# Layer 0 of a four-layer convolution chain: one entry for three 64x64 matmul steps, and the planned order made anew

## The chip, the cores and the metric

The kernel runs on one core of a Trainium2 chip. The metric is device time in microseconds (us) of one execution; of several runs the median is given.

## The reference, cut to what matters

An input of 8 images, 128 channels, 96x96, passes four layers, each of the form x = x + conv(group_norm(x)). Only layer 0 is touched here, a deformable convolution:

```python
def _dcnv4_forward(x, dw_w, dw_b, gn_w, gn_b, om_w, om_b):
    x1 = depthwise 3x3 convolution of x + dw_b
    x1 = gelu(normalised over the image, gn_w, gn_b)
    om = einsum('nhwc,oc->nhwo', x1, om_w) + om_b     # 8 groups x 9 taps x (2 offsets, 1 mask)
    ...
    # each of 9 taps per group is read bilinearly at its offset place, times its mask
    out = jnp.sum(samp * mask[..., None], axis=4)
...
x = x + _L0_conv_ref(_gn(x), ...)      # layer 0
x = x + _L1_conv_ref(_gn(x), ...)      # 3x3
x = x + _L2_conv_ref(_gn(x), ...)      # depthwise with signs
x = x + _L3_conv_ref(_gn(x), ...)      # a scan over rows
```

## The kernel before, in words

**Work of layer 0.** An image is cut into BR = 6 chunks of 16 rows, so there are 48 chunks. A chunk's result is the sum of 25 shifted copies of the normalised image, each times a weight map. For each shift VectorE (DVE) multiplies a map row by a shifted slice (`pr`, line 1077), and TensorE (PE) adds the product into PSUM `ps_s` with 16 matmuls on 32x32 tiles (`add_all`, line 1031). From chunk 6 on one product in 25 is made by GpSimd (POOL, line 1085), in the last chunk seven. There are three `pr` buffers: product k+3 can't start before the add of product k has read its own. After 25 adds ScalarE (ACT) moves `ps_s` out (`y`, line 1111), and the first add of the next chunk (the residual, `sdd`) waits for that, as there is one `ps_s`.

**The weight maps.** POOL builds them per chunk into `wx` (lines 978 to 1012, two buffers) from "tents", ten ACT instructions on the offsets `om` (lines 943 to 952). ACT copies five rows of `wx` per chunk to PSUM for DVE (`ps_wb`, line 1054, two buffers of five products each). `om` comes from DRAM into one buffer (SP, line 922), after four projections on PE (line 899, `project`, two matmuls each into the one PSUM buffer `ps_w`), their evictions on ACT (`oe`, line 907) and their stores (line 915). A chunk's projections run some three chunks ahead, on x1 after GELU (`x1c`, line 884, loaded at line 880).

**The image ahead.** While the chunks of image i run, image i+1 is prepared: rows loaded (SP, line 502), statistics on ACT (line 604), a chain of tiny operations on DVE, PE and ACT for the group norm (lines 638 to 343), normalising on ACT (line 711), copies to DRAM (line 722), and the depthwise convolution in 12 blocks on PE. A block is three `near` taps (line 745, four 64x64 matmuls each) and three `over` taps (line 761, eight 32x32 matmuls each) into `ps_w`; ACT evicts it (line 783) and takes a square sum (line 790), SP stores it (line 799). After the 12th block a second chain of tiny operations (lines 813 to 837) gives the coefficients of the GELU, so the first projections of the next image wait for it.

**What sets the order.** The program has no dynamic order: all of it is planned in Python. Each piece is a `plan.task(engine, cost, fn, deps, prio, ...)`. `Plan.order` plays the engines against each other with the given costs, always starting the ready task of lowest `prio`, and each engine then issues its instructions in that fixed sequence. A cost, a prio or a constant has no other effect than on this sequence. `CH` is the spacing of the chunks' prios, `SLOT_AT` how early slices are loaded, `BEHIND1` how far image 1's preparation is put back, `EACH_ON_POOL` which product POOL makes, `STATS_LATE` an offset of the statistics.

Of the kernel before, what the change touches and what calls it, by code (L numbers as in the profile page):

```python
# [51 lines left out]
    return sorted(every, key=lambda s: (s[0] % NR, s[1] % NR))  # L52


CONV_COST = 0.66, 0.8
CH, SHIFT, PE_KEEP = 47.0, 8.6, 2.0
LOAD_AT, NORM_AT, COPY_AT, COPY_LATE, COPY_FROM = -140, -90, -20, 220, 52
CONV_AT, CONV_STEP, CONV_PACE = -60, 20, 1.5
X1_AT, OM_STEP, SLOT_AT = -140, 4.0, 35
BEHIND, AHEAD, CONV_BEHIND = 40, 60, 40  # L60
HOLD, BEHIND1 = False, 40
GATE, SLOTS_FROM = 12, 0
LAST_ON_POOL, EACH_ON_POOL, POOL_W = (4, 7, 10, 13, 16, 19, 22), (16,), 20
PAIR, FROM_CHUNK = 1, 6
STATS_ON_ACT, STATS_LATE = True, 0


class Buf:
# [136 lines left out]
def kernel(  # L205
# [33 lines left out]
    NB, HC = 2, P // 2  # L239
    YB, BR = 16, H // 16  # L240

    NQ, QC = 4, P // 4
# [186 lines left out]
    with ExitStack() as ph:  # L429
# [49 lines left out]
        plan = Plan()  # L479
# [95 lines left out]
        def image(i, at, before=()):  # L575
# [36 lines left out]
            prev = []  # L612
# [122 lines left out]
            for c in range(NST):  # L735
                ps = plan.buf("s" if i == 0 and c % 2 else "w")
                need = (norms[: NB * (c + 2)] if c < NST - 1 else norms) + (ready if i == 0 else [])
                prev = []

                def near(t, ps=ps, c=c):  # L740

                    r0, c0 = RP + c * RB, RS - 1 + t
                    for j in range(NB):
                        for h in range(2):
                            nc.tensor.matmul(
                                ps.tile[half(j), h, :FB],
                                dwn[half(h), j, t].rearrange("p e c -> p (e c)"),
                                xq[half(h), r0 : r0 + RB, j, c0 : c0 + W],
                                start=(t == 0),
                                stop=False,  # L750
                            )

                def over(t, ps=ps, c=c):

                    c0 = RS - 1 + t
                    for j in range(NB):
                        for p in range(2):
                            r0 = RP + c * RB + 1 - 2 * p
                            for h in range(2):
                                of = quarter(2 * h + p)  # L760
                                nc.tensor.matmul(  # L761
                                    ps.tile[quarter(2 * j + 1 - p), h, :FB],
                                    dwo[of, j, t],
                                    xq[of, r0 : r0 + RB, j, c0 : c0 + W],
                                    start=False,
                                    stop=(t == 2),
                                )

                when = at + CONV_AT + CONV_STEP * c
                for k in range(6):  # L770
                    prev = [task(
                        "PE", CONV_COST[k // 3], lambda t=k % 3, tap=(near, over)[k // 3]: tap(t), need + prev,
                        when + CONV_PACE * k + (CONV_BEHIND - BEHIND if i else 0), uses=[ps], lag=0.5,
                        shape=HC if k < 3 else QC,
                    )]
                for k in (c - 1, c, c + 1):
                    if (i, k) in free_rows:
                        free_rows[i, k] = free_rows[i, k] + prev
                x1 = plan.buf("x1")

                def evict(c=c, x1=x1, ps=ps):
                    for h in range(2):
                        nc.scalar.activation(
                            x1.tile[:, h, :], ps.tile[:, h, :FB], AF.Identity, accum_out=st1[:, h, c : c + 1]
                        )

                ev = plan.task("ACT", 1.5, evict, prev, when + 16 - AHEAD, uses=[ps, x1])
                stats1.append(plan.task(
                    "ACT", 0.97,
                    lambda c=c, x1=x1: nc.scalar.activation(  # L790
                        junk[:], x1.tile[:], AF.Square, accum_out=st1[:, 2, c : c + 1]
                    ),
                    [ev], when + 18, uses=[x1],
                ))

                def store(c=c, x1=x1):
                    for j in range(NB):
                        for p in range(2):
                            nc.sync.dma_start(
                                x1d[i, j, p].rearrange("(h c) k w -> c h (k w)", h=2)[:, :, c * FB : (c + 1) * FB],  # L800
                                x1.tile[quarter(2 * j + p), :, :],
                            )

                outs.append(plan.task("SP", 2.4, store, [ev], when + 18, uses=[x1], lag=2.2, move=1.3))
# [66 lines left out]
        def chunk(i, dy, made):  # L871
# [177 lines left out]
            for sy in range(NS):  # L1049
                wb = plan.buf("wb")  # L1050
                d, y = places[sy]
                cp = plan.task(
                    "ACT", 0.62,
                    lambda wb=wb, d=d, y=y: nc.scalar.activation(  # L1054
                        wb.tile[:, : NS * W], wx.tile[:, d, y].rearrange("p x w -> p (x w)"), AF.Identity
                    ),
                    known[sy], at + SHIFT * (sy - 1) - AHEAD, uses=[wb, wx], lag=0.1,
                )
                slot = slots[dy + sy]
                last_chunk = n == N * BR - 1  # L1060
                on_pool_k = LAST_ON_POOL if last_chunk else EACH_ON_POOL if n >= FROM_CHUNK else ()
                sx = 0
                while sx < NS:
                    shared = k in on_pool_k
                    m = PAIR if not shared and sx + PAIR <= NS and not any(k + e in on_pool_k for e in range(PAIR)) else 1
                    pr = plan.buf(("oe" if last_chunk else "oe") if shared else "pr")
                    when = at + SHIFT * sy + SHIFT / NS * sx

                    def mul(wb=wb, pr=pr, slot=slot, sx=sx, m=m):
                        rows = slot.tile[:, :, sx : sx + W]  # L1070
                        parts, *free = rows.ap
                        nc.vector.tensor_tensor(
                            pr.tile[:, :m],
                            wb.tile[:, sx * W : (sx + m) * W].rearrange("p (s w) -> p s w", s=m).unsqueeze(2).to_broadcast([P, m, GC, W]),
                            bass.AP(rows.tensor, rows.offset, [parts, [1, m], *free]),
                            ALU.mult,
                        ) if m > 1 else nc.vector.tensor_tensor(  # L1077
                            pr.tile[:, 0],
                            wb.tile[:, sx * W : (sx + 1) * W].unsqueeze(1).to_broadcast([P, GC, W]),
                            rows,  # L1080
                            ALU.mult,
                        )

                    def mul_pool(pr=pr, slot=slot, sx=sx, d=d, y=y):
                        nc.gpsimd.tensor_tensor(
                            pr.tile[:],
                            wx.tile[:, d, y, sx].unsqueeze(1).to_broadcast([P, GC, W]),
                            slot.tile[:, :, sx : sx + W],
                            ALU.mult,
                        )  # L1090

                    if shared:
                        t = plan.task("POOL", 3.65, mul_pool, [*known[sy], slot.load], when - POOL_W, uses=[wx, pr, slot], lag=0.1)
                    else:
                        t = plan.task("DVE", 0.06 + 1.66 * m, mul, [cp, slot.load], when, uses=[wb, pr, slot], lag=0.1)
                    for e in range(m):
                        k += 1
                        adds.append(plan.task(
                            "PE", 0.82,
                            lambda pr=pr, last=(k == NS * NS), e=e, shared=shared: add_all(  # L1100
                                lambda rows32, f: idr[rows32, :],
                                lambda rows32, f: (pr.tile if shared else pr.tile[:, e])[rows32, 4 * f : 4 * f + 4, :],
                                False, last,
                            ),
                            [t, adds[-1]], when + SHIFT / NS * e + 2, uses=[pr, total], lag=0.5, shape=32,
                        ))
                    sx += m
# [1012 lines left out]
```

## Time and profile before

| | |
|---|---|
| median of 9 runs | 4372.96 us (4363.4 to 4430.16) |
| the profiled execution | 4362.44 us, span 4360.7 us |
| layer 0 | from 0 to about 2325 us |
| first and last eviction of a chunk (line 1111) | 230.2 and 2315.4 us |
| layers 1 and 2, layer 3 | to about 3600 us, to the end |

In the page's fifth part a row names line, engine, operation, tiles (written <- read), shape and count, then the busy time, the mean duration of one in ns, and the idle time of its engine just before with what ended it. In the timeline a row gives start and length in us of equal instructions that follow each other; f32 matmuls show twice, so an add is x32, a near tap x8, an over tap x16, a projection x4. In the table by stretches come the stretch, then busy us of each engine, the granted PE clock, the DMA share and GB/s.

### The profile page before, as it was taken

The page shows a single profiled execution, that of the slowest core. Times are in us where ns is not written, and L with a number is a line of the kernel's source. Part 1 is how long each engine was busy: PE and PEld are TensorE (multiplying, and loading weights), DVE is VectorE, ACT ScalarE, POOL GpSimd, SP SyncE. Part 2 cuts the span into 40 slices and gives each one's busy share as a digit, 9 for nine tenths or more (in the row PEclk, how much of TensorE's full clock was granted, in tenths as well). Part 3 has the DMA queues.
Part 4 walks back from the last instruction along what each step waited for, and adds up shares of the span by engine and source line. Part 5 has one row for each costly group of instructions (what it writes and reads, how often), then busy time and mean ns, then how long its engine had stood idle before and what let it go on. Part 6 is the DMA issues. An engine that isn't in the chain of part 4 may idle for free. (4 is left out here: it accounts for less than half of the span.)

```text
span 4360.7 us, 157120 instructions
## 1 busy us (share of the span) xinstructions
PE 3946.3 (90%) x69622; PEld 2329.6 (53%) x69622; DVE 3687.9 (85%) x4493; ACT 2687.5 (62%) x4194; POOL 3253.5 (75%) x2248
## 2 busy tenths in 40 slices
PE   5598999989999899998767999899999979999999
PEld 2243443434444344443324555455555549999999
DVE  2599998999999989999994688888888868888887
ACT  3767667676677766655532687687788773333332
POOL 0388899898989889898995799899999952222222
PEclk9799999989999899999998999999999989999999
DMA  7886867768677595856422223222332222323231
GB/s 159 188 206 153 205 165 185 195 149 218 154 193 193 147 224 144 201 154 154 139 64 68 58 73 81 66 67 71 77 76 74 51 67 95 110 92 112 91 113 73
DMA packets 760177, 556.55 MB, mean 128 GB/s; under 512 B 619873, under 2 KB 742514, under 8 KB 753346
## 3 DMA queue, kind: packets, MB, share of 16 engines
q1 hardware_dynamic: 726658, 504.68, 45.6%
q10 hardware_dynamic: 32464, 40.17, 2.6%
q8 instruction: 549, 8.99, 0.9%
q0 software_dynamic: 368, 1.57, 0.1%
q14 instruction: 138, 1.13, 0.1%
HBM read 290.64 MB, written 255.66 MB: 125 GB/s over the span
## 5 line engine op out<-in xcount | busy, mean ns | idle before, releaser
L1077 DVE TENSOR_TENSOR pr<-ps_wb,xs 128x1536 f32<-128x1536 f32 x1152 | 1934.4, 1747 | 132.5 <-PE ps_s L1031 91.1
L1031 PE MATMUL ps_s<-pr,idr 32*32 32x384 f32 x36864 | 1303.2, 516 | 173.0 <-DVE pr L1077 131.8
L1031 PEld LDWEIGHTS ps_s<-pr,idr 32*32 32x32 f32 x36864 | 526.9, 105 | 748.4 <-DVE pr L1077 438.0
L1604 PE MATMUL pv_C<-dC,km 128*128 128x384 f32 x1920 | 683.6, 493 | 26.9 <-DVE vn L1627 13.7
L1970 POOL TENSOR_TENSOR xtD<-xtD,cr 128x384 f32<-128x384 f32 x192 | 192.7, 1004 | 585.5 <-ACT cr L1969 523.4
L1734 DVE SCALAR_TENSOR_TENSOR pd_C<-xqC,w2s,pd_C 128x768 f32<-128x768 f32 x546 | 554.3, 1015 | 68.5 <-ACT pd_C L1762 38.6
L1604 PEld LDWEIGHTS pv_C<-dC,km 128*128 128x128 f32 x1920 | 355.0, 190 | 322.3 <-issue 59.0
L978 POOL TENSOR_TENSOR ty<-ty,om 128x864 f32<-128x864 f32 x142 | 289.9, 2041 | 286.5 <-ACT ty L952 157.3
L1003 POOL TENSOR_TENSOR wx<-wx,tmp 128x576 f32<-128x576 f32 x284 | 403.0, 1419 | 22.3
L1590 POOL TENSOR_TENSOR dC<-ywC 128x392 f32<-128x392 f32 x384 | 357.1, 959 | 80.0 <-PE pv_C L1604 51.9
L2031 PE MATMUL ps_b<-tr,km 128*128 128x192 f32 x2304 | 407.1, 325 | 0.7 <-DVE tr L2016 0.7
L2031 PE MATMUL ps_a<-tr,km 128*128 128x192 f32 x2304 | 405.4, 324 | 0.0
L1001 POOL TENSOR_TENSOR tmp<-tx,ty 128x576 f32<-128x576 f32 x284 | 405.3, 1427 | 0.0
L1751 POOL TENSOR_TENSOR ptC<-ptC,ptC 128x768 f32<-128x768 f32 x222 | 403.3, 1830 | 1.8 <-ACT ptC L1742 1.7
L2031 PEld LDWEIGHTS ps_b<-tr,km 128*128 128x128 f32 x2304 | 380.8, 189 | 0.7 <-ACT sd_oC L1870 0.7
L2031 PEld LDWEIGHTS ps_a<-tr,km 128*128 128x128 f32 x2304 | 379.4, 188 | 0.0
L2039 ACT ACTIVATE m<-ps_b 128x192 f32<-128x192 f32 x192 | 63.5, 331 | 493.7 <-PE ps_b L2031 493.7
L899 PE MATMUL ps_w<-x1c,omg 128*108 128x384 f32 x768 | 315.7, 536 | 45.7 <-ACT x1c L884 24.9
L1742 ACT ACTIVATE ptC<-vn,wsg 128x768 f32<-128x768 f32 x318 | 286.3, 928 | 74.9 <-PE pq_C L1719 48.4
L984 POOL TENSOR_TENSOR wx<-tx,ty 128x864 f32<-128x864 f32 x142 | 290.1, 2043 | 51.6 <-ACT tx L950 39.5
L1054 ACT ACTIVATE ps_wb<-wx 128x480 f32<-128x480 f32 x240 | 136.4, 569 | 279.1 <-DVE pr L1077 239.0
L761 PE MATMUL ps_w<-xq,dwo 32*32 32x384 f32 x4320 | 298.9, 493 | 7.3 <-issue 3.7
(260 smaller groups left out, 6605.7 us busy)
## 6 DMA issues: line engine op xcount, KB each, us to landing
xs<-xnd SPq DMA_DIRECT2D x80, 800.0 KB
omd<-oe SPq DMA_DIRECT2D x96, 648.0 KB
om<-omd SPq DMA_DIRECT2D x48, 1296.0 KB
xnd<-xq SPq DMA_DIRECT2D x192, 200.0 KB
x1d<-x SPq DMA_DIRECT2D x384, 96.0 KB
x1c<-x1d SPq DMA_DIRECT2D x96, 384.0 KB
y<-y SPq DMA_DIRECT2D x192, 192.0 KB
x<-oC SPq DMA_DIRECT2D x192, 192.0 KB
```

What stands on the lines that cost most here:

```text
L761: nc.tensor.matmul(ps.tile[quarter(2 * j + 1 - p), h, :FB], dwo[of, j, t], xq[of, r0 : r0 + RB, j, c0 : c0 + W], start=False, stop=(t == 2),)
L899: nc.tensor.matmul(ps.tile[:HM, b, :FB], omg[:, m * HM : (m + 1) * HM], rows[:, f0 : f0 + FB], start=True, stop=True)
L984: lambda on, s: on.tensor_tensor(flat(wx.tile[:, v, :, 1 : NS - 1]), flat(grid(tx)), flat(grid(ty)), ALU.mult),
L1001: on.tensor_tensor(part, flat(grid(te)[:, :, ks : ks + 2]), flat(grid(ty)[:, :, ks : ks + 2]), ALU.mult)
L1003: on.tensor_tensor(to, to, part, ALU.add)
L1031: nc.tensor.matmul(total.tile[32 * f : 32 * f + 32, r, :FB], weights(rows32, f), of(rows32, f), start=first, stop=last)
L1077: ) if m > 1 else nc.vector.tensor_tensor(
L1590: lambda k=k, a=a, b=b, op=op: nc.gpsimd.tensor_tensor(d.tile[:, k], yw.tile[:, a : a + CR - 1 : 2, :], yw.tile[:, b : b + CR - 1 : 2, :], op,
L1604: nc.tensor.matmul(flat(ps), w, d.tile[:, k, :, x_ : x_ + W], start=(x_ == 0), stop=(x_ == 2))
L1734: nc.vector.scalar_tensor_tensor(view, rows8(src, t, h), w[:, t : t + 1], view, ALU.mult, ALU.add)
L1751: lambda a=parts[0], b=pt: nc.gpsimd.tensor_tensor(a.tile[:], a.tile[:], b.tile[:], ALU.add),
L2031: nc.tensor.matmul(ps[:, at_f : at_f + nf], km[:, k, t, :], tr[:, par, :, v : v + HW2], start=(t == 0), stop=(t == NT - 1),)
```

## The change: what it does

```diff
-CONV_COST = 0.66, 0.8
-CH, SHIFT, PE_KEEP = 47.0, 8.6, 2.0
+CONV_COST = 1.98, 0.65
+CH, SHIFT, PE_KEEP = 46, 8.6, 2.0
...
-X1_AT, OM_STEP, SLOT_AT = -140, 4.0, 35
+X1_AT, OM_STEP, SLOT_AT = -140, 4.0, 50
...
-HOLD, BEHIND1 = False, 40
+HOLD, BEHIND1 = False, 60
...
-LAST_ON_POOL, EACH_ON_POOL, POOL_W = (4, 7, 10, 13, 16, 19, 22), (16,), 20
+LAST_ON_POOL, EACH_ON_POOL, POOL_W = (4, 7, 10, 13, 16, 19, 22), (19,), 20
...
-STATS_ON_ACT, STATS_LATE = True, 0
+STATS_ON_ACT, STATS_LATE = True, -20
...
-                for k in range(6):
+                for k in range(4):
                     prev = [task(
-                        "PE", CONV_COST[k // 3], lambda t=k % 3, tap=(near, over)[k // 3]: tap(t), need + prev,
+                        "PE", CONV_COST[min(k, 1)], lambda k=k, near=near, over=over: over(k - 1) if k else [near(t) for t in range(3)], need + prev,
...
-                        shape=HC if k < 3 else QC,
+                        shape=QC if k else HC,
...
-                        t = plan.task("POOL", 3.65, mul_pool, [*known[sy], slot.load], when - POOL_W, uses=[wx, pr, slot], lag=0.1)
+                        t = plan.task("POOL", 2.95, mul_pool, [*known[sy], slot.load], when - POOL_W, uses=[wx, pr, slot], lag=0.1)
```

The three near taps of a block become one task, so nothing can come between them; the three over taps stay single. The other edits are new costs and constants of the plan. The number of instructions and their shapes stay the same; only the sequence on each engine changes.

PE's sequence over six chunks, as planned before and after. S is the residual add that opens a chunk, O the add of one product, n a near tap, v an over tap, p a projection, * tiny matmuls of the coefficient chains:

```
before 21 SOvOvOvOOOnOnOnOvOvOvOOnnOnOOOvOvOvOOnOnOnOOvvv
before 22 SOOOO*OO*OOOOOpOOpOOpOOOOOpO*OO*OOp
before 23 SpOOOpOOOOOpOO*OOnnOnOOvvOOOvOOpOOpOOpOp
before 24 SOOnnnvOvOvOOOnnOnOOvvOvOOpOOpOO*OOpOOpOOnnnOOvvv
before 25 SOOOnOnOnOvOvOvOOnOnOOnvOOvvOOOpOOpOOpOOOp
before 26 SOOOnnnOOvOvOvOOnOnOOnvOOvvOOOpOOpOOpOOOpOnnn
after 21 SOOOnnnOOvOvOvOOOnnnOOOvvOvOOOO*O*OOOOOpOp
after 22 SpOOOOOpOOOOOOpOO*OpO*OOOpOOOpOOnnnOOvvv
after 23 SOOOnnnOOOvvOvOOO*OpOOpOOpOOOOOOpOOnnnOOvvv
after 24 SOOOnnnOOvOvOvOOOnnnOOvOvvOOpOOpOOpOOO*OOpOnnn
after 25 SOOOvvOvOOOOOOOOnnnOOvOvOvOOpOOpOOpOOpOnnn
after 26 SOOOvvOvOOnnnOOOvvOvOOpOOOpOOOOpOOnnnOOvvv
```

From image 3 on the pattern repeats every six chunks. After the first chunk's start, the near taps stand in 183 separate runs before and in 84 after. On SP, the last two row loads of an image stood around the last store of x1 before (chunk 22: eight loads, store, `x1c` load, eight loads, all behind the stores of `y`); after, the last store and the `x1c` load come in chunk 21, ahead of the last eight loads and of the stores of `y`.

## The prediction

> **What bounds the kernel now.** I read the page first, then the table by stretches, then the waits of single engines inside layer 0, and last the timeline of one image.
>
> ```profile
> PEclk9799999989999899999998999999999989999999
> L1077 DVE TENSOR_TENSOR pr<-ps_wb,xs 128x1536 f32<-128x1536 f32 x1152 | 1934.4, 1747 | 132.5 <-PE ps_s L1031 91.1
> ```
>
> The products are the costliest group, with 132.5 us of idle time before them, two thirds of it until an add gave a buffer back. The change touches nothing after 2325 us, where layer 0 ends, so its whole effect is what these gaps do. One steady image (from the eviction of chunk 21 on) by stretch, then the waits inside layer 0 of DVE, POOL and ACT:
>
> ```profile
> 1167.00:1436.00 269.00, 246.73 (x5960) 115.81 (x5942) 249.24 (x176) 187.81 (x329) 246.92 (x164) 0.94 0.72 182
> DVE pr L1077 <- PE ps_s L1031: 89.5, 78, 4.6
> DVE pr L1077 <- ACT ps_wb L1054: 23.0, 12, 7.8
> POOL ty L978 <- ACT ty L951: 114.4, 19, 9.7
> ACT ty L943 <- DMA om<-omd: 70.0, 23, 7.7
> ```
>
> Of 269 us DVE (third) is busy 249, POOL (fifth) 247, PE (first) 247. DVE is nearest to its floor: 144 products at 1.67 us (12 take 20.06 us below) are 240.5, the tiny chains about 9. What can be won is the 18.9 us that DVE idles per image: listing its gaps, I find the boundary of the images (chunks 22 to 24) with 4.59 + 0.22 + 1.52 + 1.57, the middles of chunks with 4.9 in seven gaps (the largest 1.69), two waits for a map copy behind tents with 2.04, and three chunk ends with 1.86, 0.91 and 1.29. The largest, in the timelines of PE, DVE and SP:
>
> ```profile
> 1187.44 1.60 PE L1031 MATMUL ps_s<-pr,idr 32*32 32x384 f32 x32 [0.72 <-DVE pr L1077]
> 1192.38 2.90 PE L899 MATMUL ps_w<-x1c,omg 128*108 128x384 f32 x4 [3.34 <-DMA xq<-in_x]
> 1195.21 2.89 PE L1031 MATMUL ps_s<-pr,idr 32*32 32x384 f32 x64
> 1196.98 3.42 DVE L1077 TENSOR_TENSOR pr<-ps_wb,xs 128x1536 f32<-128x1536 f32 x2 [4.59 <-PE ps_s L1031]
> 1171.84 7.12 SPq L502 DMA_DIRECT2D xq<-in_x  x8
> 1179.05 2.36 SPq L799 DMA_DIRECT2D x1d<-x  x4
> 1182.53 1.24 SPq L880 DMA_DIRECT2D x1c<-x1d  x2
> ```
>
> The first projection of the next image stands in PE's sequence 11 products after the last convolution matmul, and PE stops 3.34 us there until `x1c` has come and passed the GELU; the store of x1 had waited on SP behind eight row loads (7.12 us of issue). Adds that were ready stand behind it, so DVE runs out of buffers.
>
> **The joined near taps.** Rows of PE, two taps alone between adds, then three taps in one run, then DVE's price:
>
> ```profile
> 1330.30 0.88 PE L745 MATMUL ps_w<-xq,dwn 64*64 64x384 f32 x8
> 1331.11 0.94 PE L1031 MATMUL ps_s<-pr,idr 32*32 32x384 f32 x32
> 1331.99 0.88 PE L745 MATMUL ps_w<-xq,dwn 64*64 64x384 f32 x8
> 1039.32 2.18 PE L745 MATMUL ps_w<-xq,dwn 64*64 64x384 f32 x24
> 1041.43 1.92 PE L1031 MATMUL ps_s<-pr,idr 32*32 32x384 f32 x64
> 1324.99 20.06 DVE L1077 TENSOR_TENSOR pr<-ps_wb,xs 128x1536 f32<-128x1536 f32 x12 [0.61 <-PE ps_s L1031]
> ```
>
> By starts, tap and add cost 0.81 + 0.88 = 1.69 us, against 1.67 for a product: a PE that is late stays late through nOnOnO. Joined, three taps take 2.11 us, and the two adds behind them 1.53 (the next over tap starts at 1042.96), so that three taps and three adds take 4.4 us instead of 5.07, and 0.65 us of lateness is paid back. The lump itself fits: after an add that ended in time PE may be some 2.4 us late (two further products, 3.34, less an add, 0.94). PE saves some 99 runs x 0.65 = 64 us, but it isn't the end of the path; only the seven gaps in the middles of chunks are, 4.9 us per image, and also the spread of the blocks helps there (three blocks in a chunk before at 24, 26 and 27; two or three after, one already in chunk 22). Some of these gaps are waits for the one `ps_w` and stay. I let half go: 2.4 us per image (0 to 4.9).
>
> **The boundary.** After, the coefficient chain stands in chunk 21, and between the last over tap and the first projection are 10 products, 17 us, one fewer than before. Before, that way took 23.5 us (1168.9 to 1192.38), of which 7.1 was the row loads ahead of the store. These now precede the block's end, so 16 to 17 us remain, about what the products cover; four statistics on ACT ahead of the GELU (0.95 us each) lie beside the coefficient chain's rest. The 4.59 + 0.22 go. In their place comes a new group, pOpSp at the end of chunk 21. Before it stood as two, pSp into chunk 23 (1.52 us of DVE idle) and pOpS into chunk 24 (1.57). I take their sum, 3.1. Bounds: at full clock (chunk 23's end, where a projection takes 1.47 from start to start, an add between two of them 1.06 and one behind them 0.67) the group is 3 x 1.47 + 2 x 1.06 + 0.67 = 7.2 us against two products and the allowance, 3.34 + 2.4, so 1.5; at half clock (2.83 for a projection and about 1.5 for an add, from 1192.38 on) 13.0, so 7.3. Two further chunk ends with vvvS get 0.9 each (before, this form cost 0 and 1.86). So 7.9 becomes 4.9: 3.0 gained (-3.1 to 6.4).
>
> PE's clock decides between those bounds, and the table by stretches shows it:
>
> ```profile
> 1173.00:1198.00 25.00, 17.09 (x330) 5.27 (x324) 20.12 (x20) 20.22 (x32) 24.61 (x17) 0.66 0.82 181
> 2153.00:2193.00 40.00, 24.76 (x832) 8.04 (x832) 39.93 (x25) 14.58 (x22) 39.22 (x27) 1.00 0.24 76
> ```
>
> With adds alone (62% busy) the clock stays at 1.00; with the tiny chains between them it fell to 0.66, with no PE gap over 1.3 us before it. The chain stays, denser, so I expect half clock in part of the group. [...]
>
> **The rest of the order.** Chunk ends elsewhere: 1.86 + 0.91 + 1.29 before; after, two pnnnS and one vvvS, no better, 0 (-4 to +2). Tents: before T8 or T9, after up to ten in a row ahead of the next copy, 0 (the second rival). SP: slices 15 us earlier in prio and `om` behind fewer row loads; every slice wait of DVE was nil in the image read, so 0. POOL's product as the 20th instead of the 17th holds an `oe` buffer three products longer; POOL waited on `oe` stores 3.0 us in all: 0 to -3 in the whole. Start: one piece shifts in chunk 0, 0 (within 5). Chunk 41 idles 7.8 us on projections at half clock; after, six stand wider apart instead of eight: half, 3.5 (0 to 7).
>
> **Sum.** 2.4 + 3.0 = 5.4 us per image, six images (1 to 6) = 32, and 3.5: 36 us off the profiled 4362.4, so 4326.5. The median of the runs lies 10.5 above that execution: 4337.
>
> **Rivals.**
> First, POOL caps it. Per image POOL works 246.9 us and waits 17.1, mostly for tents of a late `om`. If that ring keeps its waits, 264 + 2 us of small gaps is the shortest image: 3 gained instead of 5.4, 18 + 3.5 in all, 4351. Against it: the boundary's projections come some 15 products earlier, which feeds POOL's largest wait.
> Second, and slower: a map copy behind waiting tents. At 784.90 ACT waited 7.68 us for `om`, eight tents ran, the copy behind them came late, and DVE idled 5.70 us. After, ten tents run in a row (1.6 us more), so 7.3 per event. Five products per copy and two copies held give 16.7 us; less two copies (1.1), ten tents (9.1) and an eviction (0.9), a wait above some 5.3 us decides it. The mean was 70.0 / 23 = 3.0, the longest 7.7, so it is near. Once per image is 44 us, over the gain of 36: 4381; oftener, up to 4400.
> Third, more than forecast: the boundary group at 1.5 and all middle gaps gone, 4.6 + 4.9 = 9.5 us per image, 57 + 3.5 in all: 4312. For it speaks that PE is busy in chunk 22 with a block more; against it that some middle gaps are waits for `ps_w`.
> Fourth, no effect: gaps only move, as all three engines lie within 8% of the image; 4373.
>
> **How the numbers follow.** The forecast gets 0.38, POOL's cap 0.15, more than forecast 0.14, no effect 0.11, slower 0.22. A measurement can tell about 0.2%, 9 us. Of the first three, 0.03 may end inside that: faster 0.64, same 0.14, slower 0.22. The range runs from 4297 (the third rival with the vvvS ends at nothing, 11 us, and all of chunk 41, 4) to 4390 (the second with a fifth more events), leaving out under 2 in 10.
>
> **What would show it.** Right: an image of about 263 us between evictions instead of 269; no PE wait of over 1 us at line 899 for the first projection of an image; a DVE gap of about 3 us just after chunk 21's eviction; DVE's idle before line 1077 near 95 us; near taps only as x24. Wrong: PE's waits at line 899 stay; or idle for `ps_wb` well above 23.0 us and long waits at line 943 (second rival); or POOL's wait at line 978 still near 114 us with images at 266 (first). I would also be wrong if chunk 0's eviction moves from 230.2 by over 5 us.

## The result, and the profile after

The changed kernel takes 4394.63 us (median of 10 runs) against 4372.45 for the kernel before (31 runs): ratio 1.0057, 95% interval 1.0045 to 1.0069, so 0.57% slower. Forecast were 4337 us. Some executions of most kernels took 50 to 90 us longer than the rest; medians count them, the ratios leave them out, but for one of e13's (4466.16 us), without which the ratio there is about 1.010. The profiled execution of after took 4401.86 us, 7 above its median, that of before 10 below its own: the two profiles are 39 us apart, the runs 22 to 25. What follows from the profiles shows kinds and places; for sizes the runs count.

The whole loss is in layer 0. From the first eviction of a chunk to the last it took 2085.2 us before (230.2 to 2315.4) and takes 2121.4 now (235.0 to 2356.4); what comes behind took 2045.3 and takes 2043.7. From the page of after, the clock and the products:

```profile
PEclk9699999999999999999998999999999989999999
L1077 DVE TENSOR_TENSOR pr<-ps_wb,xs 128x1536 f32<-128x1536 f32 x1152 | 1934.0, 1747 | 169.7 <-PE ps_s L1031 138.0
```

The products cost the same (1934.4 before); the idle time ahead of them grew from 132.5 to 169.7 us; behind adds it grew by more than that (91.1 to 138.0), elsewhere it fell. The table by stretches, columns as in the prediction: image 1 and a steady image of after, then image 1 of before.

```profile
465.30:745.70 280.40, 243.47 (x5976) 114.82 (x5976) 252.69 (x177) 186.81 (x332) 248.19 (x163) 0.95 0.72 172
1204.60:1479.20 274.60, 244.86 (x5977) 117.86 (x5976) 251.43 (x178) 188.43 (x332) 247.22 (x162) 0.95 0.75 178
```
```profile
462.40:726.90 264.50, 239.25 (x5900) 107.38 (x5900) 248.93 (x176) 185.02 (x328) 238.80 (x158) 0.95 0.72 178
```

None of the images 1 to 6 is at the forecast 263 us. Images 1 to 6, from eviction to eviction, took 264.5, 270.5, 268.7, 269.5, 266.4, 268.9 before and 280.4, 272.8, 276.9, 274.2, 277.5, 264.5 after. Image 1, which the prediction had taken for an image like the others, lost 15.9 us, the most of all.

**Waits inside layer 0**, after (us in total, times, longest):

```profile
DVE pr L1077 <- PE ps_s L1031: 138.0, 102, 4.7
POOL ty L978 <- ACT ty L951: 71.9, 21, 8.3
POOL oe L1085 <- DMA omd<-oe: 25.8, 4, 10.1
ACT ty L943 <- DMA om<-omd: 57.8, 21, 7.6
POOL wx L984 <- ACT tx L950: 63.8, 31, 4.3
PE ps_s L1031 <- DVE pr L1077: 160.4, 218, 4.7
PE ps_s L1031 <- issue: 48.7, 34, 3.2
PE ps_w L761 <- issue: 19.5, 12, 3.5
DVE pr L1077 <- ACT ps_wb L1054: 16.2, 7, 7.4
PE ps_w L899 <- ACT x1c L884: 5.3, 8, 2.0
```

and the lines of before that the prediction did not show:

```profile
POOL wx L984 <- ACT tx L950: 37.9, 21, 3.6
POOL oe L1085 <- DMA omd<-oe: 3.0, 2, 2.0
PE ps_s L1031 <- DVE pr L1077: 128.4, 174, 4.1
PE ps_s L1031 <- issue: 39.5, 44, 2.0
PE ps_w L899 <- ACT x1c L884: 11.0, 7, 2.7
PE ps_w L899 <- DMA xq<-in_x: 6.2, 2, 3.3
PE ps_w L761 <- issue: 3.7, 4, 1.4
```

PE's waits for the projections' input fell from 17.2 to 5.3 us, those of ACT for `om` and of DVE for a map copy fell too. POOL's wait at line 978 fell by 42 us, but it waits 26 us more for tents at line 984, and 25.8 for an `oe` store, where it had waited 3.0. PE waits 32 us more for DVE's products, with nothing left to add; what grew most beside that is idle time before adds and over taps that has no releaser at all, "issue": 43.2 to 68.2 us.

**What "issue" is.** At the start of chunk 24, in the timelines of PE and DVE:

```profile
1297.87 1.69 PE L1031 MATMUL ps_s<-pr,idr 32*32 32x384 f32 x38
1302.78 3.17 PE L1031 MATMUL ps_s<-pr,idr 32*32 32x384 f32 x57 [3.22 <-issue]
1304.48 3.42 DVE L1077 TENSOR_TENSOR pr<-ps_wb,xs 128x1536 f32<-128x1536 f32 x2 [3.59 <-PE ps_s L1031]
```

PE stops in the middle of an add though its operands are there, and DVE, out of buffers, loses 3.59 us. Numbering PE's records (139244 matmuls and weight loads, 844 of its sequencer) in order, all such gaps over 0.3 us stand at one place modulo 256 (193 or 194). The page's third part has the other half:

```profile
q8 instruction: 549, 8.99, 0.9%
```

That is a DMA queue with 549 packets of 16384 bytes, one for each 256 of PE's 140088 records. Here one ran from 1299.90 to 1301.23, and PE went on 1.55 us after its end; in general PE goes on 1.4 to 1.5 us after. I read these packets as PE's instructions, fetched in blocks of 256 while it runs: the page calls the queue "instruction", there is one packet per 256 records, and the gaps stand at one place in 256 and end soon after a packet. Where a fetch starts soon, it is some 0.7 us after PE enters the block before (DMA's mean share in the 10 us around it is about 0.5); others start 3 to 5 us after (share 0.95 to 1.0); it takes 1.1 us (median). Where the start came under 1.2 us late no gap followed in either kernel, where it came 3 to 5 us late a gap followed in 33 of 59 cases before and 40 of 58 after, in the kernel after mostly where PE needed only 4.1 to 5.0 us for its 256 instructions (median 5.7). The sequence of after isn't denser as a whole, and its fetches aren't later: 121 of layer 0's 358 blocks ran in under 5 us (123 before), and 62 fetches started 3 us late or more (60 before). What grew is how often the two meet, 27 times instead of 10.

I sorted each DVE gap of layer 0 (us): a gap that an ACT instruction ended stands with ACT, any other by what PE did in the 9 us before it, late fetches first. The table says what stood near a gap, not what each kind would save.

| | before | after |
|---|---|---|
| a late fetch on PE | 29.5 | 76.7 |
| start of a chunk, without a late fetch | 42.2 | 55.6 |
| PE's wait at line 899 (the boundary) | 18.3 | 3.4 |
| copies, tents and evictions on ACT | 37.9 | 16.7 |
| the rest | 4.3 | 17.8 |
| sum | 132.2 | 170.2 |

**The boundary.** Timelines of PE, DVE and SP around the eviction of chunk 21, after:

```profile
1201.38 1.54 PE L899 MATMUL ps_w<-x1c,omg 128*108 128x384 f32 x4
1203.91 1.54 PE L899 MATMUL ps_w<-x1c,omg 128*108 128x384 f32 x4
1206.17 0.94 PE L1031 MATMUL ps_s<-xs,sdd 32*32 32x384 f32 x32 [0.72 <-ACT y L1111]
1209.63 11.74 DVE L1077 TENSOR_TENSOR pr<-ps_wb,xs 128x1536 f32<-128x1536 f32 x7 [2.52 <-PE ps_s L1031]
1187.87 1.45 SPq L880 DMA_DIRECT2D x1c<-x1d  x2
1189.73 5.88 SPq L502 DMA_DIRECT2D xq<-in_x  x8
```

The load of `x1c` now stands ahead of the eight row loads, the first projection doesn't wait, and the group pOpSp costs DVE 2.52 us where the prediction put 3.1.

**Image 1.** PE and DVE at the change from chunk 6 to 7, after:

```profile
504.89 2.18 PE L745 MATMUL ps_w<-xq,dwn 64*64 64x384 f32 x24 [0.18 <-ACT oe L907]
506.99 1.53 PE L761 MATMUL ps_w<-xq,dwo 32*32 32x384 f32 x32
510.17 5.08 DVE L1077 TENSOR_TENSOR pr<-ps_wb,xs 128x1536 f32<-128x1536 f32 x3 [1.56 <-PE ps_s L1031]
511.73 2.16 PE L745 MATMUL ps_w<-xq,dwn 64*64 64x384 f32 x18
514.47 0.87 PE L745 MATMUL ps_w<-xq,dwn 64*64 64x384 f32 x6 [0.58 <-issue]
519.25 5.08 DVE L1077 TENSOR_TENSOR pr<-ps_wb,xs 128x1536 f32<-128x1536 f32 x3 [3.99 <-PE ps_s L1031]
```

Here PE's sequence is OpOnnnvvvOOOnnnvvvS: whole blocks between two adds, some 4 us. Before, image 1 had none of these and ran nOnOnO. One in a chunk's middle costs DVE some 1.5 us, the one at the chunk's end 3.99, of which a late fetch inside it (0.58 us of PE's time) is a part.

### The profile page after: what moved, and what is told of

It is laid out like the page before. It is cut to its first block, busy times and chain, and to the rows that moved or that the text cites. A ratio compares the mean times of both kernels' runs of the same rounds, so it can differ in the third digit from the quotient of the medians.

```text
span 4400.0 us, 157115 instructions
## 1 busy us (share of the span) xinstructions
PE 3921.0 (89%) x69622; PEld 2354.0 (53%) x69622; DVE 3684.9 (84%) x4493; ACT 2688.6 (61%) x4194; POOL 3277.0 (74%) x2248
## 5 line engine op out<-in xcount | busy, mean ns | idle before, releaser
L1077 DVE TENSOR_TENSOR pr<-ps_wb,xs 128x1536 f32<-128x1536 f32 x1152 | 1934.0, 1747 | 169.7 <-PE ps_s L1031 138.0
L1031 PE MATMUL ps_s<-pr,idr 32*32 32x384 f32 x36864 | 1275.1, 513 | 217.7 <-DVE pr L1077 161.5
L1031 PEld LDWEIGHTS ps_s<-pr,idr 32*32 32x32 f32 x36864 | 534.4, 105 | 779.2 <-DVE pr L1077 466.9
L1604 PE MATMUL pv_C<-dC,km 128*128 128x384 f32 x1920 | 682.5, 492 | 27.9 <-DVE vn L1627 13.9
L899 PE MATMUL ps_w<-x1c,omg 128*108 128x384 f32 x768 | 314.0, 534 | 44.4 <-ACT x1c L884 15.6
```

Of the source, the lines that this page charges most:

```text
L899: nc.tensor.matmul(ps.tile[:HM, b, :FB], omg[:, m * HM : (m + 1) * HM], rows[:, f0 : f0 + FB], start=True, stop=True)
L1031: nc.tensor.matmul(total.tile[32 * f : 32 * f + 32, r, :FB], weights(rows32, f), of(rows32, f), start=first, stop=last)
L1604: nc.tensor.matmul(flat(ps), w, d.tile[:, k, :, x_ : x_ + W], start=(x_ == 0), stop=(x_ == 2))
```

## The experiments

All ratios are to the kernel before in the same set of runs. The theories: (1) late fetches, because PE's new sequence is denser; (2) the order itself, in certain constants or places; for the pads also (3) the chance of where a block of 256 begins.

**1 and 2. Each half of the change alone.** e1 is the join with its cost, all constants as before; e2 all constants as after, the join undone.

```diff
# e1, against before: and the loop over 4 entries
-CONV_COST = 0.66, 0.8
+CONV_COST = 1.98, 0.8
# e2, against after: and the loop over 6 entries
-CONV_COST = 1.98, 0.65
+CONV_COST = 0.66, 0.65
```

> The kernel before with the three near taps of a block as one entry of cost 1.98 us, all other costs and constants as before; the order is made anew with that. If the denser blocks of convolution matmuls are what costs (PE then passes 256 instructions faster than the next 256 are fetched), this shows most of the loss: 4385 to 4400 us, PE's idle time of unknown cause inside layer 0 (the 'issue' gaps over 0.3 us, 43.8 us before and 68.7 us after) at 60 us or more. If the other constants carry the loss (POOL's product as the 20th, slices 15 us earlier, statistics earlier), it stays at 4365 to 4376 us. If the prediction's step of the near taps holds by itself (2.4 us per image), it comes to about 4358 us.

> The kernel after with the near taps as three single entries of 0.66 us again; the over taps at 0.65 us, POOL's product as the 20th, and all other constants as after. If the constants carry the loss: 4385 to 4400 us, with DVE's idle time at the starts of chunks near 55 us (42 before, 56 after). If the join with its fetch gaps carries it: within 10 us of 4372, the issue gaps of PE near 44 us.

e1: 4414.77 us, 1.0110 (1.0094 to 1.0126). e2: 4447.59 us, 1.0184 (1.0165 to 1.0204). Both are slower than the whole change, and neither theory fits: e1 has fewer late fetches than before (35.7 us of gaps against 43.8) but 78.0 us of DVE's idle time at starts of chunks (42.2); e2 has 43.6 us of fetch gaps, and 60.1 us of idle time for the map copies (23.0). So the size of the loss doesn't follow the sum of late fetches. The order is made anew as a whole by every constant, so the halves of the change are not parts of its effect. One can't undo single constants to find a cause; what can be done is to change the sequence that was planned, or what lies around it.

**3 to 6. The place in the packets.** Matmuls of one element ahead of layer 0: 32 of them are 128 records, four each as in the adds (18432 matmuls, 73728 records): half a block (the first expectation took them for 64), and 64 of them are a whole block.

```diff
+        pad = wp.tile([1, 1], F32, name="pad")
+        nc.vector.memset(pad[:], 0.0)
...
+        w0 = plan.pools["w"].tiles[0]
+        for _ in range(32):
+            nc.tensor.matmul(w0[:1, 1, 500:501], pad[:], pad[:], start=True, stop=True)
```

> The kernel before with 32 matmuls of one element (two records each would be 64 records) ahead of layer 0's order; nothing else moves in the sequence of any engine, only the place at which PE's instructions fall into packets of 256. If the gaps of PE at every 256th instruction are fetches that come too late, the gaps move with the packets: those over 0.3 us stand at the same residue of the instruction's number, at other pieces of work, their sum changes by 5 to 25 us and the time with a part of it (over 0.2%, 9 us, in one direction or the other, or not at all if the sum stays). If the gaps belong to the order (a wait that the profile does not show), they stay at the same pieces of work, and the time is that of before within 0.1% plus 2 us for the added matmuls.

> The kernel after with the same 32 matmuls of one element ahead of layer 0. If part of the loss is where the packets of 256 instructions happened to fall, the time changes by over 9 us (4375 to 4388 if the sum of the issue gaps goes back from 68.7 to about 45 us). If the loss is in the order itself, or if dense blocks make late fetches wherever the packets fall, it stays at 4390 to 4400 with a sum of 60 to 75 us.

> The kernel after with 64 matmuls of one element ahead of layer 0, which are 256 records: a whole packet, so that every later instruction falls at the same place of a packet as without them. If it is the place in the packets that gave 17 us with 32 matmuls (4377.4 against 4394.6), the gain is gone here: 4390 to 4400 us, and the issue gaps of PE in layer 0 come to 62 to 75 us at the same pieces of work as in the kernel after. If the added matmuls help by something else (a later start, a clock that is up earlier), it stays near 4377.

> The kernel before with the same 64 matmuls (one whole packet). If the place in the packets gave the 16 us with 32 matmuls (4351.1 against 4367.0), this is 4363 to 4374 us. If something else of the added matmuls helps, it stays near 4351.

| | before | after |
|---|---|---|
| 32 matmuls | 4351.06, 0.9969 (0.9953 to 0.9985) | 4377.40, 1.0026 (1.0016 to 1.0035) |
| 64 matmuls | 4359.11, 0.9970 (0.9957 to 0.9982) | 4381.97, 1.0023 (1.0012 to 1.0034) |

The gaps moved to other pieces of work and kept their place modulo 256, so they belong to the packets. But half a block and a whole block give the same time: theory 3 falls. Both kernels gain 0.3%, and something else in the edit gave it. The loss of after stays 0.5 to 0.6% in each pair, and that with the same sum of late fetches: PE's gaps over 0.3 us behind them come to 52.1 us before and 51.8 after with 32 matmuls, 50.2 and 51.1 with 64. So the loss doesn't need more of them (theory 1 in its plain form); what can still differ is how much of them reaches DVE.

**7. The join alone, in the order of before.** The planned order is kept; the second and third near tap are issued behind the first.

```diff
-        for t in self.order():
-            t.fn()
+        done, near = self.order(), {}
+        for t in done:
+            if hasattr(t, "near"):
+                near.setdefault(t.near, []).append(t)
+        for t in done:
+            if not hasattr(t, "near"):
+                t.fn()
+            elif t is near[t.near][0]:
+                for u in near[t.near]:
+                    u.fn()
...
+                    if k < 3:
+                        prev[0].near = i, c
```

> The join alone: the order of the kernel before, unchanged on every engine, but the second and the third near tap of each block are issued directly behind the first (some 99 runs of one or two taps become one of three). Prediction's step: 2.4 us per image less (0 to 4.9), so 4353 us (4338 to 4367). Against it: fewer changes of shape make PE pass its packets of 256 instructions faster, so the issue gaps grow from 43.8 us towards 60, and the adds behind a run of three come 1.3 us later: then 4372 to 4390.

4374.98 us, 0.9997 (0.9986 to 1.0009). Its waits (add_all is line 1041 there, the products 1087):

```profile
DVE pr L1087 <- PE ps_s L1041: 97.2, 85, 4.5
PE ps_s L1041 <- issue: 41.4, 39, 2.9
DVE pr L1087 <- ACT ps_wb L1064: 27.6, 12, 7.0
```

The joined taps are worth nothing, either way. The gaps behind late fetches cost DVE 39.4 us instead of 29.5, starts of chunks 36.1 instead of 42.2. So the step of the near taps is refuted by itself, and joined taps alone did not make this sequence slower; what the join does through the plan is in e1.

**8. The chunk ends of after, one add earlier.**

```diff
+        ahead, n = {}, kind.find("OOnOOvvvS")
...
+            add, near = pe[n + 1 : n + 3]
...
+                ahead[add.number] = near
...
```

Here n is the joined entry, and what stands in `ahead` is issued ahead of that add.

> The kernel after with the near taps at the end of two chunks of three per image issued one add earlier: OOnnnOOvvv becomes OnnnOOOvvv, so that PE pays back more of its lateness before the last add of the chunk. Nothing else moves. If the run nnnOOvvvS is what makes the chunk ends dear (15 ends with 2.2 us of DVE's idle time each, 1.6 where no fetch fell into them, against 0.05 for nOnOnOOvvvS before), some 10 ends give back 0.5 to 1.5 us each: 4378 to 4390. If only the fetches make them dear, the time stays within 5 us of 4394.6.

4399.75 us, 1.0058 (1.0042 to 1.0075): nothing gained. Ten ends became nnnOOOvvvS; they cost 2.15 us each, and 8 of the 10 have a late fetch. PE's waits for `ps_w` at the near taps grew to 13.4 us (8.7 after). The run moved PE's work within a stretch that is too full; it doesn't separate the two theories.

**9 and 10. The address.** Only the tile of one element, no matmul. The tiles from `xs` on move by 32 bytes: `oe`, for one, is allocated at 214528 in SBUF instead of 214496 (by the built programs). In e10 the tile comes first in the pool, so that `xq` moves too.

```diff
+        pad = wp.tile([1, 1], F32, name="pad")
+        nc.vector.memset(pad[:], 0.0)
         plan = Plan()
```

> The kernel before with one tile of one element allocated (and set to 0 once) ahead of the tiles xs, pr, y, om, tx, ty, wx, x, x1c and oe, and no matmul added: these tiles move up by 32 bytes in SBUF, from addresses that leave 32 in a division by 64 to multiples of 64. In both runs with added matmuls, which had this tile too, DMA packets of 384 bytes took 27.7 to 28.0 ns instead of 29.6 and the time was 0.997 of before's. If the address does it: ratio 0.997 (4355 to 4363 us), the packets at 28 ns. If the added matmuls did it (by their place in PE's packets, or by a later start): within 0.1% of before, packets at 29.6 ns.

> The same tile as the first of layer 0's pool, so that the image rows xq, the near and over weights and the scratch tiles move by 32 bytes as well. If the address of a DMA's tile is what counts, the row loads of xq (384 byte packets, at 8 bytes into a row of 400) have no address of 64 either way, so little more than with the tile put later: 0.995 to 0.998. If xq's rows gain too: 0.990 to 0.995.

e9: 4354.80 us, 0.9970 (0.9953 to 0.9986). e10: 4354.56 us, 0.9967 (0.9952 to 0.9982). The address alone does it, and `xq` adds nothing. DVE's products aren't faster by it (1749 ns on average, 1747 before). In the trace the 384 byte packets of layer 0 take 27.8 ns on average instead of 29.6 and DMA is busy 63.7% of layer 0 instead of 65.6. Layer 0's queue before, its queue in e9, and e9's waits (lines 2 higher there):

```profile
q1 hardware_dynamic: 480858, 344.60, 65.6%
```
```profile
q1 hardware_dynamic: 480670, 344.48, 63.7%
```
```profile
DVE pr L1079 <- PE ps_s L1033: 72.6, 71, 3.4
PE ps_s L1033 <- issue: 30.8, 30, 2.6
```

**11 and 12. Less DMA traffic.** Of the projections' results 4 of 16 rows go out and back, of x1c 8 of 16 rows are loaded; the rest is 0, so the weight maps are not those of the reference. Every instruction keeps its place.

```diff
-    nc.sync.dma_start(x1.tile[half(j)], x1d[i, j, dy % 2, :, dy // 2 :: BR // 2, :])
+    nc.sync.dma_start(x1.tile[half(j), :8], x1d[i, j, dy % 2, :, dy // 2 : dy // 2 + 8 * (BR // 2) : BR // 2, :])
...
-    omd[n, :, m * HM : (m + 1) * HM].rearrange("y r w -> r y w"), oe.tile[:HM]
+    omd[n, :4, m * HM : (m + 1) * HM].rearrange("y r w -> r y w"), oe.tile[:HM, :4]
...
-    om.tile[:].rearrange("p a k w -> p (a k w)"),
-    omd[n].rearrange("y (g k) w -> (y g) (k w)", g=NG),
+    om.tile[: 4 * NG].rearrange("p a k w -> p (a k w)"),
+    omd[n, :4].rearrange("y (g k) w -> (y g) (k w)", g=NG),
...
+        nc.vector.memset(plan.pools["om"].tiles[0][:], 0.0)
+        nc.vector.memset(plan.pools["x1c"].tiles[0][:], 0.0)
```

> The kernel before with less DMA traffic: of the projections' results only 4 of 16 rows go to DRAM and back (oe to omd, omd to om), and of x1c only 8 of 16 rows are loaded; the rest of om and x1c is set to 0 once, so the weight maps are wrong there. Every instruction of every engine stays in its place. Estimate: DMA's share in layer 0 falls from 0.67 to about 0.45. If PE's gaps at every 256th instruction are fetches that queue behind other DMA traffic, their sum falls from 43.8 to under 20 us, and the time by 20 to 40 us (the waits for om and x1c go too). If these gaps have another cause, their sum stays at 40 to 50 us.

> The kernel after with the same traffic left out. If late fetches are what the new order pays with, they go here (from 68.7 us to under 25) and with them its loss: not over the time of before with the same traffic left out by more than 5 us, or below it by up to the forecast 36. If the order itself costs (the chunk ends nnnOOvvvS and pOpSp, waits for ps_w), it stays 10 to 25 us over it.

e11: 4288.11 us, 0.9809 (0.9784 to 0.9833). e12: 4304.68 us, 0.9855 (0.9834 to 0.9876). Waits in layer 0 of e11, then of e12:

```profile
DVE pr L1077 <- PE ps_s L1031: 51.8, 36, 2.8
PE ps_s L1031 <- issue: 7.1, 9, 1.8
ACT ty L943 <- DMA om<-omd: 5.0, 4, 1.5
```
```profile
DVE pr L1077 <- PE ps_s L1031: 71.7, 66, 3.8
PE ps_s L1031 <- issue: 9.5, 12, 1.7
ACT ty L943 <- DMA om<-omd: 4.9, 3, 1.8
```

The sum of PE's fetch gaps falls to 9.1 us in e11 (43.8) and 13.9 in e12 (68.7), with DMA's share at 0.49 and 0.51: fetches are late because of the other traffic. This is shown: PE's sequence is the same. But the loss of after doesn't go with them: 16.6 us are left by medians (20 by the ratios) of 22 (25), as there were with equal late fetches above. DVE's gaps by kind, as in the table above:

| us, before / after | late fetch | starts of chunks | line 899 | ACT | rest |
|---|---|---|---|---|---|
| as timed (the first table) | 29.5 / 76.7 | 42.2 / 55.6 | 18.3 / 3.4 | 37.9 / 16.7 | 4.3 / 17.8 |
| tiles moved, 32 matmuls | 30.2 / 53.1 | 39.8 / 54.1 | 9.9 / 2.7 | 34.8 / 10.8 | 8.9 / 20.0 |
| tiles moved, 64 matmuls | 40.2 / 55.2 | 42.3 / 57.9 | 9.1 / 4.3 | 33.6 / 13.5 | 4.4 / 23.4 |
| less traffic | 11.3 / 13.8 | 37.3 / 51.3 | 3.2 / 0.0 | 15.6 / 11.4 | 0.2 / 7.8 |

Two terms stand under all four conditions: the starts of chunks cost the new order 13 to 16 us more, and the rest (mostly PE behind without a late fetch, and its waits for `ps_w` at near taps) 8 to 19. Late fetches stand before more of DVE's idle time than in the order of before only where DMA is crowded, and there its gains (line 899, and ACT's work coming in time) are larger too; with less traffic both go together. A form of chunk end shows the two terms in one: vvvS cost 0.71 us each before (13 of them) and 2.28 after (17); with less traffic 0.75 (12) and 0.98 (17).

**13 to 15. One constant back, the steady images kept.** With BEHIND1 at 40 PE's sequence is that of after from chunk 21 on. e14 adds the edit of e12, e15 that of e9.

```diff
-HOLD, BEHIND1 = False, 60
+HOLD, BEHIND1 = False, 40
```

> The kernel after with one constant taken back: BEHIND1 at 40 again, so image 1's preparation comes 20 us earlier in prio. The order is made anew with it, but PE's sequence differs from that of the kernel after in chunks 0 to 20 alone and is the same from chunk 21 on. If the loss that is left without late fetches (16.6 us) sits in image 1 (its chunks 6 to 11 took 280.4 us after and 264.5 before), 4378 to 4386 us, with image 1 at 264 to 272 us. If it is spread over the images, 4390 to 4398.

> The same with the DMA traffic of the projections cut as before (4 of 16 rows of oe and om, 8 of 16 of x1c; the weight maps are wrong there). If image 1 holds the order's own loss: 4288 to 4294 us against 4304.7 for the kernel after and 4288.1 for the kernel before with the same traffic cut. If not: 4300 to 4308.

> A candidate: the kernel after with BEHIND1 at 40 and the tiles from xs on moved up by 32 bytes (worth 0.3% before). If image 1 holds 12 us and the address 12 us: 4368 us; under 4355, and so better than the kernel before with moved tiles, only if both theories are wrong.

e13: 4408.99 us, 1.0132 (1.0085 to 1.0179). e14: 4318.66 us, 0.9888 (0.9871 to 0.9906), 14 over e12. e15: 4390.23 us, 1.0045 (1.0030 to 1.0060), where 4368 would have confirmed both theories, and no better than after with the tiles moved (1.0023, 1.0026). Image 1 did fall to 267.6 us in e13, as forecast, but image 2 rose from 272.8 to 280.5 and image 0 from 465.3 to 472.4. The same in e14: 264.5 for image 1 (267.0 in e12), 271.3 for image 2 (257.6). The work of the images being prepared is only shoved on. So image 1 is where the new order is worst (12 to 16 us over before in four pairs of profiles), but the constant that crams it is not shown to be a cause.

**16. A version better than both?** The sequence of e7 with the tiles of e9.

```diff
# before, with both edits: e7's issue of the near taps, and
+        pad = wp.tile([1, 1], F32, name="pad")
+        nc.vector.memset(pad[:], 0.0)
```

> A candidate: the order of the kernel before with the near taps joined in place (no effect by itself, ratio 0.9997) and the tiles moved up by 32 bytes (ratio 0.997). If the two only add: ratio 0.9967, 4354 to 4360 us. If the joined taps gain where transfers are quicker and fetches less late: under 4350.

4356.95 us, 0.9981 (0.9967 to 0.9994): within what was expected if the two only add, so the join again gives nothing. The best versions are the order of before with the tiles moved (e9, e10), 0.3% faster than before and 0.9% faster than after.

## Why the prediction was wrong, step by step

**Right: the boundary.** The load of `x1c` ahead of the row loads, PE's wait at line 899 nearly gone, 2.52 us for the new group where 3.1 were taken. The projections of that group took 1.54 us each, at a granted clock of 1.00 (1196.5 to 1207 us; it was 0.50 from 1193.1 to 1196.3, just before). Half clock in part of it was wrong, to the good. Chunk 41's 7.8 us of idle time became 1.1, where half was forecast. The second rival (copies behind tents) did not come: idle time for `ps_wb` fell from 23.0 to 16.2 us. POOL's product as the 20th was priced at 0 to -3; POOL's waits for `oe` stores grew by 23 us, but no gap of DVE names POOL.

**Wrong, first: "The joined near taps".** The step gave half of 4.9 us in seven gaps in the middles of chunks to PE being late by nOnOnO, 2.4 us per image or 14 in all. e7 has exactly this edit and measures zero, within 6 us. (PE's saving of 64 us, which the sum didn't use, is a slip too: 0.65 us is the worth of a block, in which two runs go, so 99 runs fewer are some 32 us.) The term was mis-read before it was mis-sized. The line "PE ps_s L1031 <- issue: 39.5" stood in the waits of before and was not used. Sorted as above, six of the seven gaps (4.6 of the 4.9 us) follow a late fetch, the largest (1.69 us, at 1322.62) as well; so do the chunk ends priced at 1.86 and 0.91. The largest in the timelines of PE and DVE, before:

```profile
1317.44 0.86 PE L745 MATMUL ps_w<-xq,dwn 64*64 64x384 f32 x2
1319.91 1.01 PE L745 MATMUL ps_w<-xq,dwn 64*64 64x384 f32 x6 [1.61 <-issue]
1322.62 1.76 DVE L1077 TENSOR_TENSOR pr<-ps_wb,xs 128x1536 f32<-128x1536 f32 x1 [1.69 <-PE ps_s L1031]
```

PE stops after two of a near tap's eight records. Saving changes of shape wouldn't have brought the missing instructions sooner; it would have brought PE sooner to the block that was missing.

**Wrong, second: "The rest of the order", chunk ends "no better, 0 (-4 to +2)" per image.** They cost 13 to 16 us more over layer 0 in four pairs, about 2 per image and so at the dear end of the bound, and the late fetches that fall into them come on top: 24.4 us in the profile of after, 6.2 before. vvvS was priced at 0.9; it cost 0.98 where DMA was light and 2.28 as timed.

**Wrong, third: "six images (1 to 6)".** The sum multiplied the reading of one steady image by six. Image 1 has a sequence of its own, with blocks of nnnvvv between two adds, and lost 15.9 us instead of winning 5.4. The printed sequence of chunks 6 to 9 would have shown it; only chunks 21 to 26 were read.

**Not foreseen at all** were late fetches, and that fast blocks of PE can meet them more often in a new order. None of the rivals had them. Of the signs for "right" those at the boundary came true; DVE's idle time came to 169.7 us, not to 95. None of the signs listed for "wrong" came true: idle time for `ps_wb` and the waits at lines 943 and 978 fell while the time rose, and chunk 0's eviction moved by 4.8 us, within the 5 allowed. How much of the 22 us they are can't be said exactly: their part in DVE's idle time grew by 47 us in the profiles of the two kernels, by 23 and 15 in the pairs with the tiles moved (where PE's own gaps behind them had the same sum in both orders), and with less traffic, where they hardly occur, 16.6 of 22 us of loss remain, but some of the gains are gone there too. Nor is it settled what in the planner's sums makes the new starts of chunks dearer; e8 and e13 only moved the cost. So the cause of the loss is bounded, not shown: it is in the order as a whole, neither in the joined taps nor in the number of late fetches.

## What to carry to other kernels

Look for gaps of a busy PE that nothing released ("issue"), see whether they stand at a fixed number of instructions, and take them out of the gaps that a shorter PE sequence is meant to close: here they didn't shrink when near taps were joined (a sum of 45.8 us in e7, 43.8 before), and they did with less DMA traffic (9.1 in e11). Where an order is made anew, read the sequences of the images at the start as well as the steady one, and price starts of chunks before middles: by the profiles, one image times six put image 1 wrong by 21 us. A planner's constants act together, so undoing one is no experiment on its part; edit the planned sequence, or hold it and change the surroundings.

## What was not expected of the hardware

**PE's instruction fetch** shows in the traces as packets of 16384 bytes on a DMA queue, 549 for 140088 records, one for each 256. In layer 0 a fetch that came soon started some 0.7 us after the block before was entered (DMA's mean share about 0.5), others 3 to 5 us after (0.95 to 1.0); PE, which ran a block in 5.7 us (median of after), was then stopped for up to 3.5 us. With its sequence kept and 27% less DMA time (share 0.67 to 0.49) the gaps fell from 43.8 to 9.1 us.

**32 bytes of SBUF address** are 0.3% of this kernel (ratios 0.9967 to 0.9970 in four versions of before's order with the tile, 0.9981 with the taps joined; 1.0023 and 1.0026 instead of 1.0057 for after's): packets of 384 bytes take 27.8 ns instead of 29.6, and DMA is busy 63.7% of layer 0 instead of 65.6. These means are over all 384 byte packets of layer 0, many of which don't move; the single transfers were not timed apart, so why the address counts is not shown.
